# A fused macaron layer on one core: the group sums of the attention output added in PSUM on VectorE instead of on GpSimd, and the first half's last feed-forwards cut into finer steps

## The chip, the core and the metric

The kernel runs on one core of one Trainium2 chip. The time is the device time of one execution, in microseconds (us). Three runs of the kernel before gave 804.38, 804.23 and 804.96, so the median is 804.38. The profile is of one further execution. Engines are named as the profile does: PE is TensorE, PEld its weight loads, DVE is VectorE, ACT is ScalarE, POOL is GpSimd, SP issues the DMAs.

## What is computed

The input is 4 sequences of 256 tokens with 512 features, all fp32.

```
x = x + 0.5 * ffn(layernorm(x))
x = x + attention(layernorm(x)) @ wo
x = x + 0.5 * ffn(layernorm(x))
ffn(x)  = x @ W_base.T + b_base + 2 * sum over experts e of w_e * (x @ A_e.T) @ B_e.T
w       = softmax(x @ W_router.T), the best 2 of 8 experts kept, scaled to sum 1
attention: 32 query heads, 8 key/value heads of 128, rotary positions,
           causal, each token sees 128 tokens (itself among them)
```

## The kernel before

**Tiles and halves.** The 1024 tokens are 8 tiles x0 to x7 of 128 tokens, which stay in SBUF. Two halves (h = 0, 1) of four tiles are worked through one after the other. A half has 8 groups g (one key/value head with its 4 query heads) and 2 sequences b. The attention loop runs over 32 units (h, g, b), for all g of half 0, then for all g of half 1. `left` counts the units from the end: (1,4,0) has left 8, (1,6,0) has 4, (1,7,1) has 1.

**A unit.** The body at L673 is a software pipeline. It normalizes this unit's probabilities on POOL (`normalize`, L508), runs the outputs of the unit before (the queue `late`, L683), issues the next group's query products (`queries`) or key and value products, transposes this unit's probabilities on PE (`t`, copied by ACT and by DVE, which multiplies with two masks: p10 and p11, L528), makes the next unit's scores on PE (`sa`, `sb`) with their row maxima on DVE (L476 to L499), multiplies by the values on PE (`oa`, `ob`, copied to SBUF as oT by ACT, L540 and L544), and takes the next unit's exponentials on ACT (L502).

**The output products and their sums.** The product with wo is done with seven products of half-size blocks instead of eight, so weights and oT need sums first: `sums_a` (L108) on POOL makes four block sums of oT (oTs), and `sum_o_weights` (L136) four of the weights (wos); `sum_weights` (L122) does it for the queries (wqs). `outputs` (L550) runs the products in four PSUM banks: y4 goes to the second tile, y1 (products 1 and 6) to a sum z16, y2 (products 2 and 3) to the first tile, y7 (products 7 and 5) to a sum z75. ACT copies the first group's y1 and y7 to SBUF as z16 and z75 (L572), and DVE adds those of the other groups (L576). After a half's last group `add_sums` (L583) combines z16 and z75 and adds them to the two tiles, in six operations on POOL. The last unit of all, (1,7,1), uses `out_project` (L595) instead, a plain product y per tile.

**PSUM.** There are eight banks: four for products (q, k, v, oa, ob, y, and po below) and four for scores and transposes.

**The second feed-forward.** For a pair of tiles it is `ffn` (L270), cut into steps by letter. N is layer norm with its transposes: moments on DVE (L200, L202), square root on ACT (L204), reciprocal and xc on DVE (L212, L219), transposes pt on PE, the copy xn on ACT (L229). A is the narrow product pa with its copy hl on ACT (L303) and the bias on POOL (L304). R is the experts' shares, 16 small operations on DVE with one exponential on ACT (`route`, L232), and hl times the shares on POOL (L267). B is the base product po (L312, four matmuls). G transposes hl (ph, L318) with a copy ht on ACT (L320). L adds the experts' product to po (L324), adds po to the tile on DVE (L325) and stores it. M, X and T are N's parts: moments and root, xc, and transposes.

**The order.** POOL's and ACT's instructions stand as written (a manual schedule, L670); the scheduler of the framework orders PE and DVE. The second feed-forward of half 0's tiles (x0, x1 as pair 0 and x2, x3 as pair 1) waits in the queue `loose` until the last three units, where five entries are run ahead of the transposes and one behind, and in the last unit all that are left. That of half 1's tiles follows the loop in the order written at L726.

Of the kernel before, what the change touches and what calls it, by code (L numbers as in the profile page):

```python
# [13 lines left out]
AF = mybir.ActivationFunctionType  # L14
# [8 lines left out]
G = NH // NKV  # L23
# [14 lines left out]
def macaron_kernel(  # L38
# [231 lines left out]
    def ffn(tiles, tag, then):  # L270
        n, t0 = len(tiles), tiles[0]
        xf, po, state = {}, {}, {}

        def x_of(i, c):
            return xf[i // 2][:, c, ts(i % 2, P)]

        def enter(i, scaled=False):
            if i % 2 == 0:
                xf[i // 2] = sb.tile(
                    [P, KC, 2 * P], F32, tag="oT", bufs=4, name=f"xn_{tag}_{tiles[i]}"  # L280
                )
            norm(tiles[i], xf[i // 2], i % 2, tag, scaled)

        def look(i):
            measure(tiles[i], tag)

        def shape(i):
            scale(tiles[i], tag)

        def turn(i):  # L290
            enter(i, scaled=True)

        def narrow(i):
            t = tiles[i]
            if i == 0:
                state["hl"] = sb.tile([P, TPH, E * R + E], F32, tag="hl", name=f"hl_{tag}_{t0}")[:, :n, :]
            pa = score_bank(f"pa_{tag}_{t}")
            for c in range(KC):
                nc.tensor.matmul(  # L299
                    pa[:, : E * R + E], x_of(i, c), ar_sb[:, c, :],  # L300
                    start=(c == 0), stop=(c == KC - 1),
                )
            nc.scalar.copy(state["hl"][:, i, :], pa[:, : E * R + E])  # L303
            nc.gpsimd.tensor_tensor(xt[t], xt[t], half_bias, ALU.add)  # L304

        def shares():
            route(t0, n, state["hl"], tag)

        def base(i):
            po[i] = mm_bank(f"po_{tag}_{tiles[i]}")  # L310
            for c in range(KC):
                nc.tensor.matmul(po[i], x_of(i, c), wb_sb[:, c, :], start=(c == 0), stop=False)  # L312

        def gated():
            hl = state["hl"]
            pt = ps.tile([P, n, P], F32, tag="s", bufs=4, name=f"ph_{tag}_{t0}")
            for i in range(n):
                nc.tensor.transpose(pt[:, i, :], hl[:, i, : E * R], ident)  # L318
            state["ht"] = sb.tile([P, TPH, P], F32, tag="ht", bufs=1, name=f"ht_{tag}_{t0}")
            nc.scalar.copy(state["ht"][:, :n, :], pt)  # L320

        def leave(i):
            out, t = po.pop(i), tiles[i]
            nc.tensor.matmul(out, state["ht"][:, i, :], lb_sb, start=False, stop=True)  # L324
            nc.vector.scalar_tensor_tensor(xt[t], out, 0.5, xt[t], ALU.mult, ALU.add)  # L325
            then(t)

        steps = {"M": look, "X": shape, "T": turn, "N": enter, "A": narrow, "B": base, "L": leave, "R": shares, "G": gated}
        return lambda s: steps[s[0]](*(int(i) for i in s[1:]))


    qT, kT, vS, xs, z = {}, {}, {}, {}, {}

    def rope(dst, src, name):
        a = sb.tile([HD, TH], F32, tag="ra", name=f"ra_{name}")
# [172 lines left out]
    def normalize(pr, sm):  # L508
        for n in range(0, 2 * G, G):
            w = pr[:, n : n + G, :]  # L510
            nc.gpsimd.tensor_tensor(  # L511
                w, w, sm[:, n : n + G].unsqueeze(2).to_broadcast([P, G, P]), ALU.mult
            )
# [36 lines left out]
    def outputs(h, g, b, oT):  # L550

        t = h * TPH + 2 * b
        new = sb.tile([HD, 3, 2, P], F32, tag="oTs", name=f"oTs_{h}_{g}_{b}")
        lhs = sums_a(
            oT[:, :2, :P], oT[:, 2:, :P], oT[:, :2, P:], oT[:, 2:, P:], *(new[:, i] for i in range(3))
        )
        if g == 0:
            for n in (16, 75):  # L560
                z[n, b] = sb.tile([P, D], F32, tag=f"z{n}", name=f"z{n}_{h}_{b}")

        def product(which, dst):
            py = mm_bank(f"y_{h}_{g}_{b}_{which[0]}")
            for i, n in enumerate(which):
                for c in range(2):
                    nc.tensor.matmul(  # L567
                        py[:, ts(i, D // 2)], lhs[n - 1][:, c, :], weights["os", h, g][n - 1][:, c, :],
                        start=(i == 0 and c == 0), stop=(c == 1), skip_group_check=True,
                    )  # L570
            if g == 0 and dst in (16, 75):
                nc.scalar.copy(z[dst, b], py)  # L572
                return
            dst = z[dst, b] if dst in (16, 75) else xt[t + dst]
            dst = dst[:, : len(which) * D // 2]
            nc.vector.tensor_tensor(dst, py[:, : len(which) * D // 2], dst, ALU.add)  # L576

        return [
            lambda which=which, dst=dst: product(which, dst)
            for which, dst in (((4,), 1), ((1, 6), 16), ((2, 3), 0), ((7, 5), 75))  # L580
        ]

    def add_sums(h, b):  # L583

        t = h * TPH + 2 * b
        z16, z75 = z[16, b], z[75, b]
        x0, x1 = xt[t], xt[t + 1]
        lo, hi = slice(0, D // 2), slice(D // 2, D)
        for dst, other in (
            (z16[:, hi], z16[:, lo]), (x0, z16), (x0[:, hi], z75[:, hi]),  # L590
            (z75[:, lo], z16[:, hi]), (z75[:, hi], z75[:, lo]), (x1, z75),
        ):
            nc.gpsimd.tensor_tensor(dst, dst, other, ALU.add)

    def out_project(h, g, b, i, oT):  # L595
        t = h * TPH + 2 * b + i
# [24 lines left out]
    def tiles(h, b0, n):  # L621
        t0 = h * TPH + 2 * b0
        return list(range(t0, t0 + 2 * n))
# [36 lines left out]

    late, loose = deque(), deque()

    def run(queue, n):
        for _ in range(min(n, len(queue))):
            queue.popleft()()

    last = units[-1]
    ctx.enter_context(tc.manual_schedule(engines={mybir.EngineType.Pool, mybir.EngineType.Activation}))  # L670
    ahead = scores(*units[0])
    exponentials(*ahead)
    for u, (h, g, b) in enumerate(units):  # L673
        n = groups.index((h, g)) + 1
        left = len(units) - u
        rest = []
        if b == 1 and n < len(groups):
            keys(*groups[n])
        at = n + n % 2
        if at < len(groups):  # L680
            project_v(*groups[at], 2 * (1 - n % 2) + b)
        normalize(ahead[0], ahead[2])
        run(late, len(late))  # L683
        if b == 0:
            sum_o_weights(h, g)
            if n < len(groups):
                if n > 1:
                    load_o(*groups[n])
                rest = queries(*groups[n])
                while len(rest) > 2:  # L690
                    rest.pop(0)()
        else:
            if g == NKV - 2 and h + 1 < NHALF:
                sum_tokens(h + 1)
            if n + 1 < len(groups):
                sum_weights(*groups[n + 1])
                if n % 2 == 0 and n + 2 < len(groups):
                    load_v(*groups[n + 2])
        if left <= 3:
            run(loose, 5)  # L700
        p0, p1 = transposes(h, g, b, ahead[0])
        for step in rest:
            step()
        if left <= 3:
            run(loose, 1 if left > 1 else len(loose))
        if b == 0 and n + 1 < len(groups):
            load_qk(*groups[n + 1])
        if left > 1:
            ahead = scores(*units[u + 1])
        else:  # L710
            f2 = [ffn(tiles(h, b, 1), "f2", store) for b in range(BPH)]
        oT = values(h, g, b, p0, p1)
        if left > 1:
            exponentials(*ahead)
            late.extend(outputs(h, g, b, oT))
        if (h, g) == last[:2]:
            if b == 0:
                late.append(lambda: [add_sums(h, n) for n in range(BPH)])
        elif g == NKV - 1:
            late.append(lambda h=h, b=b: add_sums(h, b))  # L720
            step = ffn(tiles(h, b, 1), "f2", store)
            loose.extend(
                lambda step=step, n=n: [step(s) for s in n.split()]
                for n in ("N0", "N1 A0", "A1 R", "B0", "B1", "G", "L0", "L1")
            )
    for n, order in (  # L726
        (0, "N0 N1 A0 A1 R"), (None, 0), (0, "B0"), (None, 1), (1, "N0"), (0, "B1"), (1, "N1 A0 A1 R"),
        (0, "G L0 L1"), (1, "B0 G B1 L0 L1"),
    ):
        if n is None:  # L730
            out_project(*last, order, oT)
        else:
            for step in order.split():
                f2[n](step)
# [46 lines left out]
```

## Time and profile before

| what | us |
|---|---|
| median of three runs | 804.38 |
| the profiled execution | 804.62 |
| its span, from the first to the last instruction of the profile | 802.9 |
| PE busy | 783.9 (98%) |
| POOL busy | 481.8 (60%) |
| DVE busy | 477.6 (59%) |
| ACT busy | 225.7 (28%) |
| PE busy from 400 to 450 us | 47.1, at a mean granted clock of 0.97 |
| PE busy from 450 to 650 us | all 200, at 1.00 |
| PE busy from 676 to 782 us | 100.75 of 106, at 1.00 |

In the profile's lines L is the line of the kernel, `out<-in` the tiles written and read with buffer numbers left out, and `xN` the number of instructions. In a timeline a bracket holds the idle time before the group and the engine, tile and line that ended it. In the windows view the numbers are the busy time (and instructions) of PE, PEld, DVE, ACT and POOL, then the granted clock of PE as a share of full speed, the DMA share and GB/s.

### The profile page before, as it was taken

What the parts mean: (1) busy time and instruction counts of PE and PEld (TensorE: products, weight loads), DVE (VectorE), ACT (ScalarE), POOL (GpSimd) and SP (SyncE); (2) the same over time, 40 slices, a digit from 0 to 9 for tenths busy, and PEclk for the clock granted to TensorE, in tenths of its full rate; (3) what the DMA queues carried; (4) which work ended last, traced back from release to release, by engine and by line L of the source; (5) the groups of instructions that cost most, each with busy time, mean ns of one, the idle gap of its engine ahead of it and who ended that gap; (6) DMA issues with size and microseconds to landing.
All of it is one profiled execution on the core that took longest, in us unless ns stands there. A gap on an engine that the chain in (4) does not pass through costs nothing.

```text
span 802.9 us, 10176 instructions
## 1 busy us (share of the span) xinstructions
PE 783.9 (98%) x3524; PEld 603.7 (75%) x3524; DVE 477.6 (59%) x1198; ACT 225.7 (28%) x763; POOL 481.8 (60%) x544
## 2 busy tenths in 40 slices
PE   6999999999999999999998999999999999999998
PEld 4558878787878787888877787878787887866644
DVE  4558573748483847477664738383847465664453
ACT  4332333222222221314030332222221313044341
POOL 5312875756657474748488756657474747555551
PEclk9999999999999999999999999999999999999999
DMA  9401121212121203130211212121203030100001
GB/s 302 144 2 39 53 67 53 91 53 67 53 92 41 78 4 102 40 105 13 89 58 52 66 53 93 52 67 37 82 2 104 14 105 1 53 1 27 1 27 53
DMA packets 33556, 48.91 MB, mean 61 GB/s; under 512 B 1248, under 2 KB 14304, under 8 KB 33504
## 3 DMA queue, kind: packets, MB, share of 16 engines
q1 hardware_dynamic: 33504, 48.26, 17.9%
q8 instruction: 28, 0.46, 0.2%
q14 instruction: 24, 0.20, 0.1%
HBM read 46.15 MB, written 2.10 MB: 60 GB/s over the span
## 4 chain that ended last, share of the span: by engine, by line
PE 92%; POOL 3%; DVE 1%; DMA 1%; ACT 1%; issue 1%; SPq 0%; ACTq 0%; DVEq 0%; POOLq 0%
PE q L389 24%; PE y L567 22%; PE pp_k L363 7%; PE pv L456 7%; PE ob L543 7%; PE po_f L312 6%; PE sb L485 5%; PE sa L472 3%; PE oa L539 3%; PE t L519 2%; PE t L524 2%; PE pa_f L299 2%; PE po_f L324 1%; DMA x<-in_x_dram 1%; PE y L599 1%; PE pt_f L228 1%
## 5 line engine op out<-in xcount | busy, mean ns | idle before, releaser
L356 POOL TENSOR_TENSOR qT<-ra_q,rb_q 128x256 f32<-128x256 f32 x64 | 46.5, 727 | 146.1 <-DVE rb_q L347 146.1
L567 PE MATMUL y<-wo,oT 128*128 128x256 f32 x368 | 95.3, 382 | 0.0
L347 DVE TENSOR_TENSOR rb_q<-q,sin_sb 64x512 f32<-64x512 f32 x128 | 88.0, 688 | 1.7
L576 DVE TENSOR_TENSOR x<-y,x 128x256 f32<-128x256 f32 (+1 forms) x62 | 33.9, 546 | 90.1 <-PE y L567 90.1
L567 PEld LDWEIGHTS y<-wo,oT 128*128 128x128 f32 x368 | 70.5, 192 | 9.8
L114 POOL TENSOR_TENSOR oTs<-oT 128x256 f32<-128x256 f32 x62 | 45.4, 732 | 52.4 <-ACT oT L544 49.9
L520 ACT COPY p<-t 128x512 f32<-128x512 f32 x32 | 18.7, 586 | 204.5 <-PE t L519 204.5
L567 PE MATMUL y<-wos,oTs 128*128 128x256 f32 x248 | 64.9, 385 | 4.2 <-POOL oTs L114 4.2
L511 POOL TENSOR_TENSOR pr<-pr,sm 128x512 f32<-128x512 f32 x64 | 66.3, 1057 | 3.7 <-DVE sm L506 3.3
L576 DVE TENSOR_TENSOR z<-y,z 128x512 f32<-128x512 f32 x54 | 37.3, 690 | 52.4 <-PE y L567 52.4
L456 PEld LDWEIGHTS pv<-wv,xa 128*128 128x128 f32 x256 | 48.6, 190 | 18.1 <-issue 12.9
L389 PE MATMUL q<-xa,wq 128*128 128x256 f32 x256 | 60.8, 379 | 0.0
L502 ACT ACTIVATE pr<-pr,nm 128x128 f32<-128x128 f32 x128 | 49.8, 391 | 39.0 <-DVE nm L499 33.0
L543 PE MATMUL ob<-p,v 128*128 128x512 f32 x128 | 60.2, 593 | 0.5 <-DVE p L528 0.5
L312 PE MATMUL po_f<-wb_sb,xn_f 128*128 128x512 f32 x128 | 58.6, 596 | 2.1 <-ACT xn_f L229 2.1
L389 PE MATMUL q<-xs,wqs 128*128 128x256 f32 x256 | 60.6, 379 | 0.0
L389 PE MATMUL q<-xs,wq 128*128 128x256 f32 x256 | 60.5, 379 | 0.0
L456 PE MATMUL pv<-wv,xa 128*128 128x256 f32 x256 | 60.0, 379 | 0.0
L363 PE MATMUL pp_k<-xa,wk 128*128 128x512 f32 x128 | 57.5, 592 | 0.0
L567 PEld LDWEIGHTS y<-wos,oTs 128*128 128x128 f32 x248 | 47.2, 192 | 12.2 <-POOL oTs L114 5.8
L389 PEld LDWEIGHTS q<-xa,wq 128*128 128x128 f32 x256 | 48.5, 190 | 6.9 <-DVE mv_a L202 0.2
L389 PEld LDWEIGHTS q<-xs,wqs 128*128 128x128 f32 x256 | 48.6, 190 | 6.6
(138 smaller groups left out, 1547.8 us busy)
## 6 DMA issues: line engine op xcount, KB each, us to landing
wq<-in_wq_dram SPq DMA_DIRECT2D x16, 1024.0 KB, 5.5
wo<-in_wo_dram SPq DMA_DIRECT2D x16, 1024.0 KB, 5.0
wk<-in_wk_dram SPq DMA_DIRECT2D x16, 256.0 KB, 2.6
wv<-in_wv_dram SPq DMA_DIRECT2D x8, 512.0 KB, 3.5
x<-in_x_dram SPq DMA_DIRECT2D x8, 256.0 KB, 6.8
out_dram<-x SPq DMA_DIRECT2D x8, 256.0 KB, 2.0
wb_sb<-in_w_base_dram SPq DMA_DIRECT2D x1, 1024.0 KB, 7.4
ar_sb<-in_w_ar_dram SPq DMA_DIRECT2D x1, 272.0 KB, 4.5
```

The lines of the kernel that those rows point to most:

```text
L114: nc.gpsimd.tensor_tensor(dst, p, q, op)
L312: nc.tensor.matmul(po[i], x_of(i, c), wb_sb[:, c, :], start=(c == 0), stop=False)
L347: nc.vector.tensor_tensor(twice(b[o : o + half, :]), twice(src[i : i + half, :]), angle(sin_sb[o : o + half, :]), ALU.mult,)
L356: nc.gpsimd.tensor_tensor(old_q, a[:, :, 0, :], b[:, :, 0, :], ALU.add)
L363: nc.tensor.matmul(pp, w[:, c, :], xa[h][:, c, :], start=(c == 0), stop=(c == KC - 1))
L389: nc.tensor.matmul(bank[:, ts(j, S)], w[:, c, ts(j, HD)], x[:, c, :], start=(new and j == 0 and c == 0), stop=(c == 1), skip_group_check=True,
L456: nc.tensor.matmul(pv[:, : 2 * HD], xa[h][:, c, ts(i, P)], weights["v", h, g][:, c, :], start=(c == 0), stop=(c == KC - 1),)
L502: nc.scalar.activation(pr[:, n, :], src, AF.Exp, bias=nm[:, n : n + 1], scale=scale, accum_out=sm[:, n : n + 1],)
L511: nc.gpsimd.tensor_tensor(w, w, sm[:, n : n + G].unsqueeze(2).to_broadcast([P, G, P]), ALU.mult)
L543: nc.tensor.matmul(po, v[:, 2 * b + n, cols], p1[n], start=(n == 0), stop=(n == 1))
L567: nc.tensor.matmul(py[:, ts(i, D // 2)], lhs[n - 1][:, c, :], weights["os", h, g][n - 1][:, c, :], start=(i == 0 and c == 0), stop=(c == 1 ...
L576: nc.vector.tensor_tensor(dst, py[:, : len(which) * D // 2], dst, ALU.add)
```

## The change

It has two parts. In the first, `add_sums` moves from POOL to DVE and reads PSUM: at a half's end the last y1 and y7 aren't added into z16 and z75; instead z is added to the bank, and the bank is kept as `total`. ACT copies the total of y1 back to z16. Seven additions on DVE then combine the two banks and add them to the tiles. In half 1 the sums of sequence 1 are made as soon as unit (1,6,1) has given its outputs (it is the last that adds to them), and no longer with those of sequence 0. In the second part the queue `loose` gives way to a table by `left` with three places in a unit's body: ahead of the outputs of the unit before, ahead of the transposes, and behind them. The steps are finer: moments and roots of all four tiles go to left 8, xc of pair 0 to left 5, and so on. A square root of a constant, which loads ACT's table, stands behind the last exponentials.

```diff
             if g == 0 and dst in (16, 75):
                 nc.scalar.copy(z[dst, b], py)
-                return
-            dst = z[dst, b] if dst in (16, 75) else xt[t + dst]
-            dst = dst[:, : len(which) * D // 2]
-            nc.vector.tensor_tensor(dst, py[:, : len(which) * D // 2], dst, ALU.add)
+            elif dst in (16, 75):
+
+                end = (h, g + (b == BPH - 1)) == groups[-1] or (g == NKV - 1)
+                nc.vector.tensor_tensor(py if end else z[dst, b], py, z[dst, b], ALU.add)
+                if end:
+                    total[dst, b] = py
+                    if dst == 16:
+                        nc.scalar.copy(z[dst, b], py)
+            else:
+                dst = xt[t + dst][:, : len(which) * D // 2]
+                nc.vector.tensor_tensor(dst, py[:, : len(which) * D // 2], dst, ALU.add)
...
-        z16, z75 = z[16, b], z[75, b]
+        s16, s75, z16 = total[16, b], total[75, b], z[16, b]
         x0, x1 = xt[t], xt[t + 1]
         lo, hi = slice(0, D // 2), slice(D // 2, D)
         for dst, other in (
-            (z16[:, hi], z16[:, lo]), (x0, z16), (x0[:, hi], z75[:, hi]),
-            (z75[:, lo], z16[:, hi]), (z75[:, hi], z75[:, lo]), (x1, z75),
+            (s75[:, lo], z16[:, lo]), (s75[:, lo], z16[:, hi]), (s16[:, hi], z16[:, lo]),
+            (x0, s16), (x0[:, hi], s75[:, hi]), (x1, s75), (x1[:, hi], s75[:, lo]),
         ):
-            nc.gpsimd.tensor_tensor(dst, dst, other, ALU.add)
+            nc.vector.tensor_tensor(dst, other, dst, ALU.add)
...
+    loose = {
+        8: ("0M0 0M1 1M0 1M1", "", ""), 5: ("0X0 0X1", "", ""), 4: ("0T0 0T1 0A0 0A1 0R", "", ""),
+        3: ("", "0B0 0B1", "0G 1X0 1X1"), 2: ("0L0 0L1 1T0 1T1 1A0 1A1 1R", "", ""),
+        1: ("1B0 1B1", "", "1G 1L0 1L1"),
+    }
+
+    def fill(left, place):
+        for step in loose.get(left, ("", "", ""))[place].split():
+            slow[int(step[0])](step[1:])
...
         normalize(ahead[0], ahead[2])
+        fill(left, 0)
         run(late, len(late))
...
-        if left <= 3:
-            run(loose, 5)
+        fill(left, 1)
         p0, p1 = transposes(h, g, b, ahead[0])
         for step in rest:
             step()
-        if left <= 3:
-            run(loose, 1 if left > 1 else len(loose))
+        fill(left, 2)
...
             exponentials(*ahead)
+            if left == 2:
+                nc.scalar.activation(root, eps, AF.Sqrt)
             late.extend(outputs(h, g, b, oT))
-        if (h, g) == last[:2]:
+        if (h, g) == groups[-1]:
             if b == 0:
-                late.append(lambda: [add_sums(h, n) for n in range(BPH)])
+                late.append(lambda: add_sums(h, 0))
         elif g == NKV - 1:
             late.append(lambda h=h, b=b: add_sums(h, b))
-            step = ffn(tiles(h, b, 1), "f2", store)
-            loose.extend(
-                lambda step=step, n=n: [step(s) for s in n.split()]
-                for n in ("N0", "N1 A0", "A1 R", "B0", "B1", "G", "L0", "L1")
-            )
+            slow[b] = ffn(tiles(h, b, 1), "f2", store)
+        elif (h, g) == groups[-2] and b == BPH - 1:
+            late.append(lambda h=h, b=b: add_sums(h, b))
+    f2 = [ffn(tiles(last[0], b, 1), "f2", store) for b in range(BPH)]
     for n, order in (
-        (0, "N0 N1 A0 A1 R"), (None, 0), (0, "B0"), (None, 1), (1, "N0"), (0, "B1"), (1, "N1 A0 A1 R"),
-        (0, "G L0 L1"), (1, "B0 G B1 L0 L1"),
+        (0, "N0 N1"), (None, 0), (0, "A0 A1 R B0"), (None, 1), (1, "N0"), (0, "B1"),
+        (1, "N1 A0 A1 R"), (0, "G L0 L1"), (1, "B0 G B1 L0 L1"),
     ):
```

More of the change, by code (lines that the diff above doesn't have):

```diff
@@ L329, in ffn @@
         return lambda s: steps[s[0]](*(int(i) for i in s[1:]))
-    qT, kT, vS, xs, z = {}, {}, {}, {}, {}
+    qT, kT, vS, xs, z, total = {}, {}, {}, {}, {}, {}
     def rope(dst, src, name):
@@ L657, in macaron_kernel @@
     load_o(*groups[1])
-    late, loose = deque(), deque()
+    late, slow = deque(), {}
     def run(queue, n):
@@ L667, in run @@
             queue.popleft()()
+    loose = {
[6 more added lines that the diff above has]
+            slow[int(step[0])](step[1:])
     last = units[-1]
-    ctx.enter_context(tc.manual_schedule(engines={mybir.EngineType.Pool, mybir.EngineType.Activation}))
+    ctx.enter_context(
+        tc.manual_schedule(engines={mybir.EngineType.Pool, mybir.EngineType.Activation})
+    )
     ahead = scores(*units[0])
@@ L709, in macaron_kernel @@
             ahead = scores(*units[u + 1])
-        else:
-            f2 = [ffn(tiles(h, b, 1), "f2", store) for b in range(BPH)]
         oT = values(h, g, b, p0, p1)
```

## The prediction

> **What bounds the kernel now.** I read the page first. TensorE is busy nearly all the time, so only its idle time, and time in which it runs slowly, can be won.
>
> ```profile
> span 802.9 us, 10176 instructions
> PE 783.9 (98%) x3524; PEld 603.7 (75%) x3524; DVE 477.6 (59%) x1198; ACT 225.7 (28%) x763; POOL 481.8 (60%) x544
> ```
>
> Then the list of waits, for PE alone (engine and line, whose result it waited for, total us, times, longest):
>
> ```profile
> PE pt_f L228 <- ACT xc_f L217: 6.5, 1, 6.5
> PE y L567 <- POOL oTs L114: 4.2, 4, 2.9
> PE po_f L312 <- ACT xn_f L229: 2.1, 3, 0.7
> PE y L567 <- ACT oT L544: 1.1, 2, 0.7
> PE ob L543 <- DVE p L528: 0.5, 1, 0.5
> PE oa L539 <- ACT p L520: 0.3, 1, 0.3
> ...
> ```
>
> The 6.5 is the start of the program, which the change leaves alone. With the PE timeline I found where the others are. One is long, in unit (1,0,0), just after half 0 ends (start, us, group):
>
> ```profile
> 421.27 1.03 PE L567 MATMUL y<-wo,oT 128*128 128x256 f32 x4
> 425.24 2.02 PE L567 MATMUL y<-wos,oTs 128*128 128x256 f32 x4 [2.93 <-POOL oTs L114]
> 427.04 1.87 PE L567 MATMUL y<-wo,oT 128*128 128x256 f32 x4
> 428.75 1.03 PE L567 MATMUL y<-wo,oTs 128*128 128x256 f32 x4
> ```
>
> The next group should start 0.86 after 421.27; it starts 3.97 after, so 3.11 is lost. Then two groups take 1.80 and 1.71 from start to start instead of 0.86: another 1.79. The windows view gives the cause of that, a granted clock (the number before the last two) of 0.53:
>
> ```profile
> 421.90:425.30 3.40, 0.47 (x3) 0.07 (x1) 0.20 (x1) 0.76 (x5) 3.16 (x5) 1.00 0.00 0
> 425.20:428.80 3.60, 3.56 (x9) 2.85 (x10) 0.69 (x1) 0.00 (x0) 3.44 (x4) 0.53 0.00 0
> ```
>
> So this stall costs 3.11 + 1.79 = 4.90. The POOL timeline says why oTs is late: the sums L593 of unit (0,7,0), 410.93 to 417.6, then four weight sums (wqs), and only then oTs, whose input the ACT copy had written by 418.88 + 0.59 = 419.47.
>
> ```profile
> 410.93 0.73 POOL L593 TENSOR_TENSOR z<-z 128x256 f32<-128x256 f32 x1
> ...
> 417.60 1.26 POOL L114 TENSOR_TENSOR wqs<-wq 128x512 f32<-128x512 f32 x1
> ...
> 422.86 0.72 POOL L114 TENSOR_TENSOR oTs<-oT 128x256 f32<-128x256 f32 x1
> ```
>
> The other ten on that list lie between 678 and 773. Three examples from PE's timeline:
>
> ```profile
> 678.50 1.13 PE L567 MATMUL y<-wos,oT 128*128 128x256 f32 x4 [0.68 <-ACT oT L544]
> 713.81 1.99 PE L312 MATMUL po_f<-wb_sb,xn_f 128*128 128x512 f32 x4 [0.67 <-ACT xn_f L229]
> 751.09 1.13 PE L567 MATMUL y<-wos,oT 128*128 128x256 f32 x4 [0.46 <-ACT oT L544]
> ```
>
> The ten are 0.68, 0.41 (680.9), 0.67, 0.43 (732.2), 0.68 (738.8), 0.46, 0.42 (753.5), 0.29 (764.4), 0.48 (766.0), 0.73 (772.6): 5.25 idle. Each loses more than its idle time: about 0.16 because a group's shown length is that much over its start-to-start pitch (ob 1.88 against 1.72), and 0.10 because the first group behind it is longer (1.13 against 1.03). 5.25 + 10 x 0.26 = 7.85; from starts alone I get 8.0. All there is to win is 4.9 + 8.0 = 12.9.
>
> **Part 1, the sums at half 0's end.** Removed: 12 POOL operations (units (0,7,0) and (0,7,1)), per unit four of 128x256 at 0.73 and two of 128x512 at 1.27. Added per unit on DVE: seven operations and, on ACT, one copy at 0.59 (L572's row). DVE's nearest rows: 128x512 from PSUM 0.69 (L576), PSUM to PSUM 0.70 (L407 q<-q,v), 128x256 0.40. So 5 x 0.40 + 2 x 0.69 = 3.4 per unit. The operation with PSUM in and out at 128x256 has no row; between 0.37 (the fastest x<-y) and 0.70, I take 0.40, as its wide relative costs no more in PSUM. [...]
>
> POOL: normalize ends at 410.98, then wqs 410.98 to 416.3. oTs can start at 419.5, and its third step s2, which PE needs, ends 419.5 + 3 x 0.8 = 421.9, while PE wants it at 422.13. The stall is gone; next late is the ACT copy, with 0.2 to spare. DVE in (0,7,1): total of y1 409.8 to 410.5, copy to 411.1 (the next sum waits for it, with x<-y2 behind, which isn't ready before 411.5), p0's products delayed to 414.3 to 415.9 (ob wants them at 417.0 and 417.8), masked scores 416.2 to 418.4 instead of 416.6, nm at 419.3 and 419.9: exponentials start at 419.4 behind ACT's own copy anyway. Banks: each unit's two totals stay in PSUM until the sums have read them; at 412.8 and 417.4 they are free, wanted at 417.0 (ob) and 421.3. In (1,0,0) the last sum ends at 430.1 and u<-q6 is ready at 429.9. No new wait. **Gain 4.9**, between 4.4 and 4.9.
>
> [...] The trace shows the halving after 2.93. [...]
>
> **Part 2, half 0's last feed-forwards.** The same matmuls, elsewhere; the four stores go with their last steps, on an SP queue whose last load (wo of group (1,7)) is ahead of them in both orders, so they hold up nothing. Moments and square roots go to unit (1,4,0): a table load 1.28 and four of 0.29 in ACT's pause of 5.7 before p1c. A load for exp then stands before the exponentials of (1,4,1), which are late by 1.28. In the like unit at 413 normalize could end at 411.8 instead of 410.98, and transposes want it at 413.04 and 413.48. In the trace the activation begins 0.02 after a load, so no more is to be charged; the cover, 2.06, is used up only past that. Over the program loads fall from 14 to 12.
>
> Now PE's walk, unit by unit in the built order, in the profile's times and with its durations.
>
> (1,6,0): ob ends at 677.66; the two pt (0.43 each) fill 0.87 of the wait for oT, y starts 678.53. s2 still lands at 680.9, so a wait of 0.64 stays where 0.41 was (cost left about 0.75). Two pa (0.94 each) follow y2's first half at 682.7; xn copies end at 682.0 and 682.5. Queries then start 1.86 later than before. Shares (DVE, 16 x 0.2) end near 689.7, POOL's hl product behind them, then wos 690.4 to 695.9, wanted at 708.
>
> (1,6,1): eight po (6.86) end at 721.25, where before had 723.09. lb products and pt between ob and y cover the oT and oTs waits. pa at 731.4 wants xn behind the exponentials at 731.5 (0.2 left).
>
> (1,7,0): DVE's shares and sums interleaved end at 742.2, p11 at 741.2, ob wants it at 742.4. POOL waits for shares until 740.7, then wos_7 (5.4) until 746.8; y_7_0 wants it at 750.1 since eight po stand before it. oT and oTs waits are covered by the same po.
>
> (1,7,1): po_2 and po_3 hold two of four banks, so y2 takes y4's bank and y7 y2's; x<-y2 stands on DVE behind a sum that waits for ACT's copy, ends 755.3, y7 wants it at 755.28 (0.25 left). oa and ob have ph and lb products between, so the 0.29 and 0.48 vanish. Six more sums, two leaves and two bn lie before xc_4 on DVE: y7 ends 757.2, bn 762.9, square root (table loaded ahead) 763.4, xc_4 764.2, pt_4 wants it at 764.3 (0.2 left). A y product stands behind pt_4 and covers xn. y_7 then ends near 775.0 against 781.88. What follows has the same order on all engines and waits little before (PE loses 0.1 in all there, by its starts), so it moves as it is.
>
> Left: 0.75 + 0.2 + 0.25 + 0.2 = 1.4. **Gain 8.0 - 1.4 = 6.6**, between 3 and 8.0.
>
> Sum: 4.9 + 6.6 = 11.5. The profiled execution took 804.62 (span 802.9 and 1.7 around it), so 793.1; against the median 804.38, 792.9. I say 793.0.
>
> **Rivals.** A: DVE, not POOL, becomes late in the last two units. For: xc_4 and y7's bank have no slack, and some 22 dependent operations stand in that stretch. An operation on its forerunner's output starts about 0.1 behind its end (L407 to L345), an independent one 0.09 before. If each cost 0.15 more than I summed, 3.3 is lost: 796.3. Against: small operations follow each other at 0.205 in the trace even when dependent. B: the first stall only shrinks, because wqs still stands before oTs. For it wqs would have to start over 3 us later than 411; its weights were issued at 397.7 and land 5.6 later, so this is unlikely. If half of it stays, 795.5; if all, 797.9, as though the sums were not what held POOL. C, slower than before: wos_7, which now waits behind POOL's hl product, and so behind DVE's shares, comes too late for y_7_0. Its slack is 3.3; past that each us costs PE one, and past about 3 of waiting 1.8 more for the clock. It loses all 11.5 only if shares end some 13 us late (3.3 + 11.5 - 1.8), near 754. Shares have waited at most on ACT's hl copies, 3.7 in the trace, so it is remote.
>
> **Numbers.** The likeliest has 0.65 (791.4 to 794.5), A 0.20, B 0.08, C 0.03; 0.04 for a wait that I haven't named, faster still or just the same. The range runs from all gaps gone (804.38 - 12.9 = 791.5, and 0.1 for rounding) to A with a little more, 797.2. Faster by over 0.2% (1.6 us, about what a measurement of this kernel can tell from no change) 0.96, within 0.01, slower 0.03.
>
> **What would show it.** PE's timeline without the 2.93 wait, and 1.0 granted where 0.53 was; POOL with oTs right behind ACT's oT copy; no wait of po on xn except at the first pt_4 if at all; one wait of about 0.6 on oTs in (1,6,0). Wrong would be a wait of PE for DVE above 1 us in the last two units (A), a wait on wos (C), or a 0.5 clock anywhere in the loop.

## The result and the profile after

The kernel after took 792.82 us (median of five runs, 791.97 to 793.14), the kernel before in the same comparison 804.23 (five runs, 802.81 to 804.96). The ratio is 0.9861, with a 95% interval of 0.9847 to 0.9876: faster by 11.4 us, where 11.5 had been forecast and 793.0 named. The profiled execution took 792.82, span 791.1, so 11.8 less span than the profiled execution before.

The page of the kernel after: PE has lost 4.5 us of busy time with the same 3524 matmuls, near the 1.79 at half clock and the ten times 0.26 around waits that the prediction had counted; POOL has given up 21 us and DVE has taken 13.

```profile
PE 779.4 (99%) x3524; PEld 602.2 (76%) x3524; DVE 490.9 (62%) x1226; ACT 225.4 (28%) x766; POOL 460.4 (58%) x520
```

PE's waits in the kernel after (total us, times, longest). Of the eleven waits above 0.2 between 420 and 780, one is left, the second row; the first row is the start of the program, and the third was there before:

```profile
PE pt_f L228 <- ACT xc_f L217: 6.9, 2, 6.5
PE y L567 <- POOL oTs L114: 0.6, 1, 0.6
PE po_f L324 <- ACT ht_f L320: 0.2, 1, 0.2
```

At the end of half 0, PE's timeline of the kernel after goes on without a break, 0.86 from start to start, and the windows view grants 1.00 where it had granted 0.53:

```profile
421.13 1.03 PE L567 MATMUL y<-wo,oT 128*128 128x256 f32 x4
421.99 1.03 PE L567 MATMUL y<-wos,oTs 128*128 128x256 f32 x4
```

```profile
421.00:424.40 3.40, 3.40 (x18) 2.98 (x17) 1.33 (x3) 2.10 (x10) 3.29 (x4) 1.00 0.00 0
```

POOL's timeline of the kernel after has the reason. The weights' sums now follow `normalize` at once, at 410.79, and POOL stands idle for 3.28 behind the last of them until ACT has written oT, so oTs is as early as its input allows:

```profile
414.85 1.27 POOL L114 TENSOR_TENSOR wqs<-wq,wqs 128x512 f32<-128x512 f32 x1
419.40 0.73 POOL L114 TENSOR_TENSOR oTs<-oT 128x256 f32<-128x256 f32 x1 [3.28 <-ACT oT L544]
```

The tail, from PE's timeline of the kernel after: the y group that waited for ACT's oT and the po group that waited for xn start with no bracket, and one bracket is left.

```profile
673.50 1.10 PE L567 MATMUL y<-wos,oT 128*128 128x256 f32 x4
676.06 1.13 PE L567 MATMUL y<-wos,oTs 128*128 128x256 f32 x4 [0.60 <-POOL oTs L114]
709.54 7.03 PE L312 MATMUL po_f<-wb_sb,xn_f 128*128 128x512 f32 x16
```

To compare the two traces I took every matmul's time to the next start, less the median of its kind, and summed the excess; below, this is called a loss by starts. Before: 4.9 at the first stall, 8.0 between 676 and 782, 0.1 behind it. After: 0, 1.15 and 0.1. That is 4.9 + 6.9 = 11.8, the whole difference of the spans.

### The profile page after: what moved, and what is told of

It is laid out like the page before. It is cut to its first block, busy times and chain, and to the rows that moved or that the text cites. A ratio compares the mean times of both kernels' runs of the same rounds, so it can differ in the third digit from the quotient of the medians.

```text
span 791.1 us, 10173 instructions
## 1 busy us (share of the span) xinstructions
PE 779.4 (99%) x3524; PEld 602.2 (76%) x3524; DVE 490.9 (62%) x1226; ACT 225.4 (28%) x766; POOL 460.4 (58%) x520
## 4 chain that ended last, share of the span: by engine, by line
PE 96%; DMA 2%; DVE 1%; ACT 0%; POOL 0%; SPq 0%; issue 0%; DVEq 0%
PE q L389 24%; PE y L567 24%; PE pv L456 7%; PE ob L543 7%; PE pp_k L363 7%; PE po_f L312 6%; PE sb L485 5%; PE sa L472 4%; PE oa L539 3%; PE t L519 2%; PE t L524 2%; PE po_f L324 2%; PE pa_f L299 2%; DMA cos_sb<-in_cos_dram 1%; PE y L606 1%; PE pt_f L228 1%
## 5 line engine op out<-in xcount | busy, mean ns | idle before, releaser
L576 DVE TENSOR_TENSOR z<-y,z 128x512 f32<-128x512 f32 x46 | 31.7, 689 | 36.6 <-PE y L567 36.5
```

## The experiments

All times are medians, compared with runs of the kernel before on the same chip: 804.34 for the first four kernels, 803.69 to 803.92 for the others.

**Part 1 alone.** The kernel before with the change's sums (both hunks in `product` and `add_sums`) and with their new place; the feed-forward steps stay as they were.

```diff
-            late.append(lambda: [add_sums(h, n) for n in range(BPH)])
+            late.append(lambda: add_sums(h, 0))
...
+        elif (h, g) == groups[-2] and b == BPH - 1:
+            late.append(lambda h=h, b=b: add_sums(h, b))
```

> Part 1 alone: the sums on DVE in PSUM, half 0's last feed-forwards left where they were before. TensorE's order is that of before. Two separate parts (my theory): the stall after half 0 with its slow clock goes, 4.9 us, and nothing in the tail but at most the two waits at 764 and 766 (some 1.3 us), which stand behind moments that wait for POOL's sums: 798.0 to 799.4. If POOL's relief were what opens the tail as well: 793 to 795. If the PSUM banks that the totals hold make new waits where the base products are made as late as before: above 800.

Measured: 798.83 (six runs), ratio 0.9941 (0.9926 to 0.9955), 5.5 faster. PE's waits in its trace:

```profile
PE po_f L312 <- ACT xn_f L229: 2.1, 3, 0.7
PE y L567 <- POOL oTs L114: 1.3, 3, 0.4
PE y L567 <- ACT oT L544: 1.1, 2, 0.7
```

The 2.9 has left the oTs row (4.2 in four before, 1.3 in three now), and the rows on xn and oT stand untouched. So the first stall belongs to part 1 and the waits of the tail to part 2, but for one: the 0.48 of ob on DVE's p has also gone here. In the kernel before, DVE's moments stand ahead of p and waited for x from POOL's sums until 763.28; here DVE makes these sums itself and the moments begin at 756.45. By starts PE loses 6.0 less from 380 us on in this trace, so the 5.5 agrees with both removed waits, though the medians alone can't tell it from the 4.9 of the stall (the interval is 3.6 to 6.0).

**Part 2 alone.** The kernel after with the six additions on POOL of the kernel before.

```diff
-            nc.vector.tensor_tensor(dst, other, dst, ALU.add)
+            nc.gpsimd.tensor_tensor(dst, dst, other, ALU.add)
```

> Part 2 alone: the finer steps, the sums on POOL in SBUF as before. Two separate parts: the stall of 4.9 us after half 0 stays in full (2.9 of waiting, then a granted clock near 0.5), the tail gains less than the 6.6 of the prediction, since x4 and x5 get their sums on POOL (six operations, some 6 us, where DVE takes 3.4) right before the last feed-forward: 798 to 800. If the tail's gain doesn't need the sums on DVE: 797.5. If the finer steps are worth nothing alone: 804.

Measured: 800.20 (nine runs), ratio 0.9958 (0.9945 to 0.9971), 4.1 faster. This is just outside the 798 to 800 that I expected. The parts alone make 5.5 + 4.1 = 9.6, not the 11.4 of both. Each of these has an interval of about 1 us either way, so the times alone hardly show a difference; the trace does. The stall after half 0 is there in full, and by starts PE loses 3.6 in the tail, where the kernel before loses 8.0 and the kernel after 1.15: part 2 wins 4.4 there alone, and 6.9 with part 1. PE's waits have a row that neither the kernel before nor the kernel after has:

```profile
PE y L567 <- POOL wos L119: 1.2, 1, 1.2
```

The row is rival C in small: with the sums of half 1 still on POOL, they stand, from 740.30 on, between hl times the shares and the sums of the last group's weights. These start at 745.97, in the kernel after at 737.55; this trace runs 4.5 behind by then, so they are 3.9 later:

```profile
745.97 1.28 POOL L119 TENSOR_TENSOR wos<-wo 128x512 f32<-128x512 f32 x1
```

**Only another order on POOL.** If what held PE at 422 was the place of wqs in POOL's queue, it should be enough to put wqs behind oTs in that one unit. The kernel before, with this alone:

```diff
-                sum_weights(*groups[n + 1])
+                if (h, g) != (0, NKV - 1):
+                    sum_weights(*groups[n + 1])
...
             late.extend(outputs(h, g, b, oT))
+            if (h, g, b) == (0, NKV - 1, 1):
+                sum_weights(*groups[n + 1])
```

> Before, with one thing changed: in unit (0,7,1) the four sums of the query weights stand behind the four of oT on POOL. No sum moves to another engine. My theory, that the stall is a matter of what stands ahead of oT's sums in POOL's queue: the wait of 2.9 and the slow clock go, 799.3, as in part 1. If POOL is short of time there, so that the sums must leave it, the wait comes back a few us later (at the query products, or at the transposes of unit (1,0,1)) and the time stays at 802 to 804.

Measured: 803.41 (14 runs), ratio 1.000 (0.9989 to 1.001). This was a miss for my theory, which said 799.3; the other reading that I had written down, 802 to 804, came. The wait on oTs is gone, but one of nearly the same length has come 12 us later (PE's timeline, then DVE's, of this kernel):

```profile
437.96 1.97 PE L389 MATMUL q<-xa,wqs 128*128 128x256 f32 x8 [2.84 <-DVE v L407]
```

```profile
432.69 0.69 DVE L200 BATCH_NORM_STATS2 st_f<-x 128x6 f32<-128x512 f32 x1 [5.47 <-POOL x L593]
...
435.52 0.69 DVE L200 BATCH_NORM_STATS2 st_f<-x 128x6 f32<-128x512 f32 x1 [1.92 <-POOL x L593]
...
436.35 0.67 DVE L407 TENSOR_TENSOR u<-q,p1c 128x512 f32<-128x512 f32 x1
```

The sums of unit (0,7,1) now stand behind wqs on POOL. DVE waits for them with its moments, and the query sums u and v, which PE needs, are queued behind the moments. From 419.4 to 442.2 POOL has no gap in that trace. So the cause at half 0's end isn't only one bad place in the queue: POOL is full for longer than the late step, this order passes the lack on, and taking the sums off POOL ended it. That no order at all would do is not shown. DVE stood idle for 5.47 ahead of the first moments, while the inputs of u had come from PE by 429.94; u and v ahead of the moments on DVE is a rival that no run here tests.

**The sums on DVE, but in SBUF.** The kernel after with the six formulas of before, on z16 and z75 in SBUF, no bank held and no copy on ACT. It tells the engine from the reading of PSUM.

```diff
-            nc.gpsimd.tensor_tensor(dst, dst, other, ALU.add)
+            nc.vector.tensor_tensor(dst, dst, other, ALU.add)
```

> After, with the sums on DVE but in SBUF: z16 and z75 are added to as before, and the six operations of before run on DVE, without ACT's copy and without banks held. If reading PSUM is worth nothing and only the engine counts: 792.8 within 0.3. If the copy and the held banks cost something: 792.2 to 792.6. TensorE's order differs in one place: the last product y7 of unit (1,7,0) stands ahead of the transposes, where it waits for the bank of y2, so I expect 0.8 more: 793.6.

Measured: 793.01 (four runs), ratio 0.9869 (0.9851 to 0.9886), 0.2 from the kernel after and inside its spread. Reading PSUM brings nothing that a run can show; what part 1 wins comes with the sums leaving POOL. I had expected 0.8 more for the last y7 of (1,7,0), standing ahead of the transposes and waiting for a bank; no such wait is in the list of this trace. By starts, PE loses 0.9 more in it (some 0.2 ahead of each of ob and oa among it), which the medians neither confirm nor deny.

**How long a pause slows the clock.** My sum charged 1.79 for the clock behind the first stall. To test that price I put the stall back, in steps: the kernel after with 7, 8, 9, 10 or 15 additions on POOL that nobody needs, ahead of oT's sums of unit (0,7,1).

```diff
+        if (h, g, b) == (0, NKV - 1, BPH - 1):
+            for _ in range(7):
+                nc.gpsimd.tensor_tensor(new[:, 0].rearrange("p c q -> p (c q)"), half_bias[:, : 2 * P], half_bias[:, : 2 * P], ALU.add)
```

> The kernel after, with seven additions of 128x256 on POOL (0.73 each, 0.81 from start to start) that nobody needs, just ahead of oT's sums of unit (0,7,1). They start when wqs ends, 416.3, and end at 422.0; s2 then lands at 424.4 where PE wants it at 422.1, so PE loses about 2.3. If a stall of that length leaves the clock alone: 792.8 + 2.3 = 795.1, granted clock 1.0 behind it. If the clock halves behind any stall of some 2 us: 1.8 more, 796.9. If POOL has no slack behind it in group (1,0), further waits appear and it is more than either.

> The same with ten additions: 416.3 + 8.1 = 424.4, s2 at 426.8, PE loses about 4.7. [...] If the clock stays at 1.0 it is 797.5, and what slowed the kernel before is something else.

> The kernel after with fifteen unneeded additions on POOL ahead of oT's sums of (0,7,1). Ten gave a wait of 3.12 and 796.49 in the run whose clock stayed at 1.0, 799.88 in the one that it slowed longest. Five more at 0.68 make the wait 6.5 and the time 796.5 + 3.4 = 799.9 if the clock stays up. [...]

> The kernel after with eight unneeded additions on POOL, which gives a pause of PE near 1.06 + 0.68 = 1.75, between the 1.06 that never slowed the clock and the 2.93 that mostly did. [...] If any pause above 1 us can do it, a third of the runs or more are at 796.9.

> The same with nine, a pause near 2.4. [...] If a pause of nearly 3 us is needed, all are at 795.8; if any pause above 1 us is enough, most are at 797.5.

| additions | PE's wait in the trace | median us | runs with a mean clock of 0.998 or less |
|---|---|---|---|
| 0 (after) | none | 792.82 | 0 of 5 |
| 7 | 1.06 | 794.40 | 0 of 4 |
| 8 | 1.75 | 794.72 | 0 of 4 |
| 9 | 2.44 | 796.58 | 3 of 5 |
| 10 | 3.12 | 796.75 | 3 of 4 |
| 15 | 6.54 | 801.89 | 10 of 10 |

Of seven and ten I had expected PE to lose 2.3 and 4.7 ahead of oTs, and by the starts it lost 1.2 and 3.3: I had spaced the additions at 0.81, the pitch of POOL's steps that depend on each other, and these follow each other at 0.68. Seven and eight show a wait without any slowing. With nine, the two runs at a full clock took 795.33 and 795.71, the other three 796.58, 797.78 and 797.79. With ten I had expected the halving in every run, 792.8 + 4.7 + 1.8 = 799.3, and one run of four, at 796.49, was without it; the longest, 799.88, was the profiled one. Its windows view (the clock is the third number from the end) shows a clock below 1.00 from the slice at 424 to the one at 430, and 1.00 behind them:

```profile
422.00:424.00 2.00, 0.88 (x5) 0.42 (x3) 0.63 (x2) 1.24 (x7) 1.84 (x4) 1.00 0.00 0
424.00:426.00 2.00, 0.00 (x0) 0.00 (x0) 0.00 (x0) 0.00 (x0) 1.79 (x3) 0.73 0.00 0
426.00:428.00 2.00, 2.00 (x5) 1.64 (x6) 0.00 (x0) 0.00 (x0) 1.97 (x3) 0.50 0.00 0
428.00:430.00 2.00, 2.00 (x6) 1.55 (x5) 1.13 (x2) 0.59 (x1) 0.75 (x1) 0.50 0.00 0
430.00:432.00 2.00, 2.00 (x7) 1.61 (x6) 0.47 (x1) 0.00 (x0) 0.00 (x0) 0.56 0.00 0
432.00:434.00 2.00, 2.00 (x11) 1.77 (x10) 1.47 (x3) 0.00 (x0) 1.30 (x2) 1.00 0.00 0
```

With fifteen, 799.9 was the time for a clock that stays up, and no run was below 801.51. The kernel before agrees: of its 52 runs in these comparisons 39 had a mean clock of 0.998 or less, median 804.35, and 13 had 0.999 or 1.0, median 802.83. So the price of the halving is about 1.5 in a run, and the pause of 2.9 pays it three times in four (in part 2 alone, which keeps this pause, 8 runs of 9 had such a clock).

**Product 2 ahead of product 6.** What is left in the kernel after is the 0.60 in the body of (1,6,0). Product 2 needs no oTs and could stand before product 6, which does. In a first try I gave the new order to the outputs of unit (1,6,0); but they run in the body of (1,6,1), since a unit's outputs are made in the next one.

> The kernel after, with unit (1,6,0)'s outputs in another order: product 2, whose operands are there, stands between products 1 and 6, with a bank of its own, so that s2 is wanted 0.86 later. My account says that the wait of 0.60 and the 0.16 of lengths around it are all that is lost there: 792.8 - 0.8 = 792.0, and PE loses 0.4 in all from 676 to the end. If the products behind (3 and 7) then wait for POOL in their turn, nothing is won: 792.8.

Measured: 792.54 (four runs), ratio 0.9857 (0.9839 to 0.9876). The wait of 0.60 at 676.12 is still in its trace, so this run says nothing of the idea and shows how far two kernels with the same waits differ: 0.3. The second try has the outputs of (1,5,1):

```diff
+        def two_products():
+            banks = [mm_bank(f"y_{h}_{g}_{b}_{n}") for n in (1, 2)]
+            for i, which in enumerate(((1, 2), (6, 3))):
+                for py, n in zip(banks, which):
+                    for c in range(2):
+                        nc.tensor.matmul(
+                            py[:, ts(i, D // 2)], lhs[n - 1][:, c, :], weights["os", h, g][n - 1][:, c, :],
+                            start=(i == 0 and c == 0), stop=(c == 1), skip_group_check=True,
+                        )
...
+        if (h, g, b) == (NHALF - 1, NKV - 3, 1):
+            return [lambda: product((4,), 1), two_products, lambda: product((7, 5), 75)]
```

> The kernel after, with the outputs of unit (1,5,1), which are the ones that run in the body of (1,6,0), in another order: product 2 between products 1 and 6, in a bank of its own. The wait of 0.60 on oTs and what goes with it (0.86 in all) should be gone: 792.8 - 0.8 = 792.0, PE's losses from 676 to the end 0.4 instead of 1.2. If products 7 or 3 then wait for POOL in their turn, nothing is won: 792.8.

Measured: 791.11 (five runs, 790.71 to 792.00), ratio 0.9843 (0.9829 to 0.9856), the fastest kernel here. In PE's timeline eight matmuls on raw operands stand where four did, and no bracket is left:

```profile
673.10 1.89 PE L590 MATMUL y<-wo,oT 128*128 128x256 f32 x8
674.82 1.03 PE L590 MATMUL y<-wos,oTs 128*128 128x256 f32 x4
```

By starts, PE loses 0.38 from 380 to the end, where the kernel after loses 1.24: the 0.86 expected. The medians differ by 1.7; the rest lies in the first 380 us, where the two kernels have the same code and this trace happens to lose 1.4 less. The intervals of the two ratios overlap, so the gain of 0.86 is shown by the traces, not by the times.

**Without the square root that loads the table.** My walk of (1,7,1) had 0.2 between xc_4 and pt_4 "with the table loaded ahead". Here it is not:

```diff
-            if left == 2:
-                nc.scalar.activation(root, eps, AF.Sqrt)
```

> The kernel after without the square root of a constant in unit (1,7,0), so ACT's table is loaded where the root of x4 needs it. My sum left 0.2 between xc_4 and pt_4 with the table loaded ahead. If the load of 1.28 waits for the moments, the chain is 1.28 longer, and with the product that the scheduler now puts ahead of pt_4 (0.43) some 0.65 is lost: 793.5. If the load starts as soon as ACT is free, it lies in ACT's pause, and nothing is lost: 792.8.

Measured: 793.89 (four runs), ratio 0.9872 (0.9851 to 0.9894), 1.1 more than the kernel after. ACT's timeline of this kernel:

```profile
758.40 1.28 ACT L204 ACT_TABLE_LOAD   x1
759.69 0.29 ACT L204 ACTIVATE sd_f<-mv_f,eps 128x1 f32<-128x1 f32 x1
```

Neither of my two reasons was quite it. The load doesn't wait for the moments, which end at 758.90 on DVE, but it can't use ACT's pause either, since it stands behind the copy of oT, which ends at 758.38. In the kernel after the root starts 0.42 behind the same copy, here 1.31 behind it. Besides, the y product that stood between pt_4 and po there now stands ahead of pt_4 and no longer covers xn: PE waits 1.01 for it. The intervals of the two ratios overlap, but by starts PE loses 2.4 from 380 us on where the kernel after loses 1.2: the load ahead is a real piece of part 2, worth some 1.1.

## Why the prediction was right, point by point

**Part 1's mechanism** was right. PE's 2.93 on oTs was POOL's lateness, and taking the sums off POOL ended it; rival B (the stall stays because wqs stands before oTs) did not come. But my reading of the POOL timeline, that oTs is late because the sums and wqs stand before it, told only half. The run with another order shows that its place wasn't all: POOL was full for 23 us, and the wait came back at the next step that others needed.

**Part 1's size**, "3.11 + 1.79 = 4.90", holds for the profiled execution. As a forecast of the median it was right as well, since three runs in four of the kernel before (39 of 52) pay for the clock, but the term is a chance, not a price: the other 13 kept a mean clock of 0.999 or 1.0. Rival C's "past about 3 of waiting 1.8 more" was an estimate from this one stall; with nine additions, 3 runs of 5 had the lower clock behind a wait of 2.44.

That 11.5 met 11.4 so closely has luck in it. Of the five runs of the kernel before, two took 802.8, the time of runs without the halving. With one more of these the median, and the gain, would have been 1.4 smaller.

**The costs on DVE** were right. The addition of 128x256 within PSUM, for which I had taken 0.40 between 0.37 and 0.70, takes 0.43, and p0's products lie at 414.17 to 415.77 where I had 414.3 to 415.9. No wait came of the two banks held. My reason to add in PSUM lay in two rows of the kernel before: an addition of 128x512 takes 0.68 in SBUF (xs<-xa, L372) and 0.69 from PSUM (L576), so little could be saved. The SBUF version, 793.01 against 792.82, shows no gain either; it needs no copy, since z lies in SBUF already, so a version that first copies y to SBUF is not tested.

**Part 2** was right in mechanism and nearly in size: 8.0 - 1.4 = 6.6 predicted, 8.0 - 1.15 = 6.9 by the starts. The one wait of 0.64 on oTs in (1,6,0) is there with 0.60, though it costs 0.86 by the starts (0.76 ahead of the group, 0.10 in its longer first matmul) and not 0.75. y7's bank was put at 0.25 and lost 0.17. The 0.2 for pa is 0.03. The 0.2 for pt_4 is not there. The root comes at 758.11, where I had 763.4 in the times of the kernel before, 758.4 in those of this trace, which is 5.0 ahead in the tail; what is late instead is po behind xn, by 0.13.

**Rival A**, DVE late in the last two units, did not come; PE has no wait on DVE in the kernel after. **Rival C** did not come either, but it was nearer than I said. The wos of the last group was summed by 742.8; I had 746.8, which is 741.8 in the times of this trace. PE took it at 745.30, so the slack was 2.5 and not 3.3. With the sums still on POOL wos is 3.9 later; 3.9 - 2.5 is the 1.4 that PE loses there by starts, 1.2 of it the wait, without a slower kernel. So the slack was enough only because part 1 empties POOL for part 2. The prediction gave each part its own gain, which holds for the sum of both but not for part 2 alone.

## What to carry to other kernels

When an engine that is 60% busy is named in a wait, look at the stretch and not at the share: if its queue is full from the late step to the next one that others need, another order may only move the stall, as it did here, where time was won when work left the engine. Before crediting an edit with a special way of access (here the reading of PSUM), run the plain version on the same engine. A step to be moved ahead of a wait must be looked for in the unit in whose body it runs, which in a pipeline isn't the unit in its name.

## What the runs showed of the hardware

In these kernels a pause of PE could cost more than its length, because the granted clock was lower behind it in some runs. By the length of the pause in the trace, the runs with a mean clock of 0.998 or less were: none of 8 with pauses of 1.06 or 1.75, 3 of 5 at 2.44, 8 of 14 at 2.84 (the other order on POOL), 39 of 52 at about 2.9 (the kernel before), 3 of 4 at 3.12, all 10 at 6.54.

So from 2.44 to 3.12 one and the same kernel came out both ways. The trace with the other order on POOL is of a run without the slowing. Its windows view shows 1.00 in the stretch with the pause of 2.84 and in the one behind it:

```profile
434.70:438.00 3.30, 0.46 (x3) 0.09 (x2) 2.24 (x5) 0.00 (x0) 3.22 (x3) 1.00 0.00 0
438.00:442.00 4.00, 4.00 (x23) 3.59 (x24) 3.89 (x6) 0.58 (x1) 3.84 (x5) 1.00 0.02 4
```

What decides it in a single run is not shown here. Ahead of the runs with eight and nine additions I had estimated 795.1 without a slowing for eight, and for nine a slowing in about half of the runs, with 795.8 or 797.5; the runs with eight had a median of 794.72, none of them slowed, and 3 of 5 with nine were slowed.

How long the clock stayed low differed as well, in one trace each. In slices of 2 from 420 on, the windows view has it below 1.00 in three with nine additions (0.80, 0.50, 0.85), in four with ten (above) and in five with fifteen (0.92, 0.50, 0.50, 0.50, 0.87).

In the trace with ten additions on POOL, those of 128x256, which don't read each other's results, follow each other at 0.68, and the four of oT's sums behind them at 0.80 to 0.81, though each of these shows 0.72.
